# Key-norm roots on ACT, expert masks in pairs, and other small DVE and POOL instructions replaced, in a two-layer decoder block with its own instruction planner

## The chip, the cores and the metric

The kernel runs on one core of a Trainium2 chip. The core's engines work side by side, each through its own queue in order: TensorE (PE in the profile, with PEld for its weight loads), VectorE (DVE), ScalarE (ACT), GpSimd (POOL) and SyncE (SP, which here only issues DMAs). The metric is the device time of one execution in microseconds, lower is better. Before the change it was 1558.11 us, the median of three runs (1554.93, 1558.11 and 1562.21 us).

## The reference

The input `x` is 4 x 512 tokens of width 128, `ctx` is 4 x 154 rows of width 128. Six sublayers follow one another, and each ends in a layer norm of (input + sublayer):

```
x = LN(x + attn1(x))            # 16 heads of width 8, gated weights, softmax over 512 keys
x = LN(x + xattn(ctx, x))       # 16 heads of width 64, keys = LN(ctx) rows and LN(x) rows, 666 keys
x = LN(x + moe0(x))             # 16 experts of width 64, the best two, plus a shared expert
x = LN(x + delta(x))            # delta rule, 16 heads of width 64:
                                #   K = K / max(norm(K), 1e-12)
                                #   W += beta * (v - W k) k^T ; o = W q, token by token
x = LN(x + cross(x, ctx, mask)) # one head, 154 masked keys
x = LN(x + moe1(x))             # 8 experts of width 512, the best one: sum over e of mask_e * gelu(x W1[e] + b1[e])
                                #   then @ Wo + bo + x, an inner layer norm, and the outer one
```

A softmax needs the maximum of its scores subtracted; a matrix product in full precision is made here of three fast products of high and low parts.

## The kernel before, in words

The whole kernel is a program for a planner that stands in the kernel itself (class `_Plan`, lines 127 to 564). The sublayer functions do not issue instructions. They record operations, each with an engine, a cost in the planner's own model, the tiles that it reads and writes, and a rank. `run` (line 363) then goes through them like a list scheduler: for the engine whose next operation could start soonest it takes the operation with the lowest key (ready time plus `RANK` times the rank, plus `TILING` where PE would have to change the shape of its tile, plus `TABLE` where ACT would have to load another function table), places its tiles in arenas of SBUF and PSUM, and issues it. So the order on every queue comes out of costs, ranks, capacities (`cap`, line 1983) and the sizes of the arenas (`SB`, `SR`, line 735). The tables `R1` to `HOLD` (lines 1916 to 1981) hold one rank per piece of work. `keep_up` (line 506) puts a filler matmul (line 2042) where the planner sees PE idle or little used. Operations recorded as `pl.any` go to whichever of two engines can start them first.

The sublayers overlap. Seen from PE, the run has five stages: attn1 of the first batch with little else (about 0 to 160 us), attn1 and the cross attention attn2 of the four batches (160 to 850 us), moe0 and the start of the delta rule (850 to 1000 us), the delta rule with the cross layer (1000 to 1400 us), and moe1 at the end.

The places that the change touches, with their lines before:

- `two_parts` (line 793). A row's maximum is subtracted inside the score product, as two bf16 parts (high part and rest). DVE makes them with three reductions over small SBUF tiles. `attn1` (line 944) calls it 16 times; `attn2` (line 1174) calls it 32 times, after one more reduction that joins the maxima of the two halves of the keys.
- `few_k` (line 1157). Attn2's keys are 26 + 5 x 128. The 26 are handled apart, and DVE adds the high and low parts of 32 key columns for them, 32 times, both operands in SBUF.
- `norm` (line 782). For every layer norm DVE gathers mean and variance, POOL adds eps and takes the power -0.5 (`stats`, line 772), then POOL negates the mean and multiplies it by the root, and ACT applies scale and bias. There are 54 calls.
- `prepare` (line 1512). For each of the delta rule's eight units (128 tokens of two batches) POOL raises the squared key norms, 128x32 numbers, to the power 0.5; `phalf` is a tile of 0.5.
- `moe1` (lines 1865 to 1870). For each expert a small matmul spreads the token's mask over 128 partitions, and DVE multiplies it with the two parts of x (128x256 each). There are eight experts in eight half batches.

## Time and profile before

| | |
|---|---|
| profiled execution, device time | 1555.95 us |
| its span, first to last instruction | 1554.2 us |
| mean granted TensorE clock | 0.966 |
| PE busy | 1466.7 us, 94% |
| DVE busy | 1128.7 us, 73% |
| POOL busy | 893.6 us, 57% |
| ACT busy | 753.6 us, 48% |
| fillers on PE | 84 |
| function table loads on ACT | 8 |

The device time is 1.75 us above the span. Busy time of PE includes the fillers, and a matmul that runs at a lower granted clock counts as busy for longer. The rows by form give, for instructions of one shape, the total and the mean of one; their idle column is the time that the engine stood still just before them, with what ended it. Tiles of the planner's arenas have only the arena's name in the profile: `arena_sm` holds tiles of up to 64 numbers per partition, `arena_sr` the matmul operands in parts, `arena_sb` the rest, `arena_mr` weights first and other tiles later, `arena_ps` PSUM. Nearly all instructions carry the line of the planner's helper (L634), so the shape tells what they are.

### The profile page before, as it was taken

What the parts mean: (1) busy time and instruction counts of PE and PEld (TensorE: products, weight loads), DVE (VectorE), ACT (ScalarE), POOL (GpSimd) and SP (SyncE); (2) the same over time, 40 slices, a digit from 0 to 9 for tenths busy, and PEclk for the clock granted to TensorE, in tenths of its full rate; (3) what the DMA queues carried; (4) which work ended last, traced back from release to release, by engine and by line L of the source; (5) the groups of instructions that cost most, each with busy time, mean ns of one, the idle gap of its engine ahead of it and who ended that gap; (6) DMA issues with size and microseconds to landing.
All of it is one profiled execution on the core that took longest, in us unless ns stands there. A gap on an engine that the chain in (4) does not pass through costs nothing. (4 is left out here: it accounts for less than half of the span.)

```text
span 1554.2 us, 38252 instructions
## 1 busy us (share of the span) xinstructions
PE 1466.7 (94%) x15610; PEld 1004.8 (65%) x15610; DVE 1128.7 (73%) x2213; ACT 753.6 (48%) x1520; POOL 893.6 (57%) x1075
## 2 busy tenths in 40 slices
PE   6899999999999999999999998898999999999997
PEld 3355545545464454556544997787888788878886
DVE  6877787887678867677787777866776877665653
ACT  3657655665655756555455354253524444133311
POOL 6011465455574566578578547787787788761221
PEclk7878999999999999999999999999999999999999
DMA  3000001001010100002100607112322032210000
GB/s 117 9 22 8 8 9 37 1 16 36 1 37 1 26 27 15 23 4 89 29 29 2 139 2 164 42 32 44 57 57 47 13 57 57 52 47 5 8 8 11
DMA packets 106853, 53.84 MB, mean 35 GB/s; under 512 B 81261, under 2 KB 92525, under 8 KB 106677
## 3 DMA queue, kind: packets, MB, share of 16 engines
q1 hardware_dynamic: 106677, 51.40, 14.2%
q8 instruction: 122, 2.00, 0.5%
q14 instruction: 54, 0.44, 0.1%
HBM read 41.19 MB, written 10.09 MB: 33 GB/s over the span
## 5 line engine op out<-in xcount | busy, mean ns | idle before, releaser
L634 PE MATMUL arena_ps<-arena_sr 128*128 128x256 f32 (+6 forms) x3824 | 607.9, 375 | 31.7 <-DVE arena_sm L634 11.8
L634 PE MATMUL arena_ps<-arena_sb 64*64 64x64 f32 (+11 forms) x7744 | 579.6, 310 | 23.3 <-issue 5.9
L610 POOL TENSOR_TENSOR arena_sb<-arena_sb 128x1024 f32<-128x1024 f32 (+3 forms) x210 | 399.2, 1910 | 313.0 <-ACT arena_sb L634 191.6
L634 PEld LDWEIGHTS arena_ps<-arena_sr 128*128 128x128 f32 (+2 forms) x3824 | 417.1, 191 | 235.5 <-DVE arena_sm L634 65.5
L634 ACT ACTIVATE arena_sb<-arena_ps 128x512 f32<-128x512 f32 (+1 forms) x758 | 389.8, 571 | 263.8 <-PE arena_ps L634 249.1
L634 DVE TENSOR_REDUCE arena_sm<-arena_ps 128x2 f32<-128x668 f32 (+3 forms) x392 | 364.6, 952 | 103.3 <-PE arena_ps L634 98.3
L634 PEld LDWEIGHTS arena_ps<-arena_sb 64*64 64x64 f32 (+6 forms) x7648 | 337.7, 141 | 147.8 <-issue 88.6
L634 POOL TENSOR_TENSOR arena_sb<-arena_sb 128x30 f32<-128x30 f32 (+15 forms) x422 | 216.0, 512 | 32.4
L596 ACT COPY arena_sb<-arena_ps 128x512 f32<-128x512 f32 (+3 forms) x237 | 134.5, 575 | 184.2 <-PE arena_ps L634 163.4
L634 DVE TENSOR_TENSOR arena_sr<-arena_ps,arena_sr 128x256 fp32r<-128x256 f32 (+3 forms) x240 | 101.2, 464 | 53.6 <-PE arena_ps L634 45.5
L634 POOL TENSOR_SCALAR arena_sm<-arena_sm 128x2 f32<-128x2 f32 (+3 forms) x116 | 26.5, 228 | 193.2 <-DVE arena_sm L634 163.7
L634 DVE TENSOR_TENSOR arena_sb<-arena_ps,arena_sb 128x512 f32<-128x512 f32 (+3 forms) x133 | 83.1, 654 | 53.9 <-PE arena_ps L634 46.8
L634 PE MATMUL arena_ps<-arena_sr,arena_mr 128*128 128x512 f32 (+2 forms) x384 | 95.7, 383 | 0.8 <-DVE arena_sr L634 0.4
L634 DVE TENSOR_TENSOR arena_sb<-arena_ps,arena_sm 64x512 f32<-64x512 f32 (+1 forms) x116 | 77.7, 685 | 25.4 <-PE arena_ps L634 19.9
L634 PE MATMUL arena_ps<-arena_sb,arena_sm 64*128 64x512 bf16 (+2 forms) x512 | 90.4, 440 | 1.3 <-DVE arena_sb L598 0.5
L634 PEld LDWEIGHTS arena_ps<-arena_sr,arena_mr 128*128 128x128 f32 x384 | 64.2, 195 | 16.7 <-issue 5.1
L634 ACT CAST arena_sr<-arena_ps 128x334 fp32r<-128x334 f32 (+3 forms) x112 | 49.3, 463 | 45.0 <-PE arena_ps L634 44.4
L598 DVE COPY arena_sb<-arena_ps 128x512 f32<-128x512 f32 (+2 forms) x73 | 47.2, 648 | 30.4 <-PE arena_ps L634 28.9
L610 DVE TENSOR_TENSOR arena_sb<-arena_sb 128x1024 f32<-128x1024 f32 (+3 forms) x37 | 54.6, 1479 | 18.7 <-POOL arena_sb L610 8.8
L610 POOL TENSOR_TENSOR arena_sr<-arena_sb,arena_sr 128x512 fp32r<-128x512 f32 (+2 forms) x30 | 47.7, 1597 | 34.4 <-ACT arena_sr L634 23.9
L634 POOL TENSOR_TENSOR arena_sm<-arena_sm,phalf 128x32 f32<-128x32 f32 x8 | 43.5, 5441 | 23.1 <-ACT arena_sb L596 17.4
L634 ACT ACTIVATE x_in<-arena_sb,arena_sm 128x128 f32<-128x128 f32 x80 | 35.0, 487 | 44.8 <-POOL arena_sm L634 38.2
(113 smaller groups left out, 1237.6 us busy)
## 6 DMA issues: line engine op xcount, KB each, us to landing
arena_sb<-s_cd SPq DMA_DIRECT2D x20, 256.0 KB
arena_sb<-s_ald SPq DMA_DIRECT2D x7, 512.0 KB
s_td<-arena_sb SPq DMA_DIRECT2D x7, 512.0 KB
arena_mr<-s_cd SPq DMA_DIRECT2D x12, 256.0 KB
s_ald<-arena_sb SPq DMA_DIRECT2D x20, 128.0 KB
arena_sb<-s_td SPq DMA_DIRECT2D x20, 128.0 KB
arena_sb<-in_f_w_dram SPq DMA_DIRECT2D x4, 512.0 KB
s_ald<-arena_mr SPq DMA_DIRECT2D x12, 128.0 KB
```

The costliest lines, as they stand in the source:

```text
L596: nc.scalar.copy(dst.real(), src.real())
L598: nc.vector.tensor_copy(dst.real(), src.real())
L610: eng.tensor_tensor(dst.real(), x.real(), y.real(), op)
L634: f(*(v.real() if isinstance(v, _View) else v for v in args), **{k: v.real() if isinstance(v, _View) else v for k, v in kw.items()},)
```

## The change

- `two_parts` becomes a copy to bf16 and a subtraction. Attn2's joining of maxima becomes one minimum of two negated tiles, so its four reductions become three instructions, and attn1's three become two.
- `few_k` is copied by ACT out of PSUM, from the same product that the key parts are made of.
- In `norm`, POOL's two last steps become one DVE instruction.
- The root of the key norms is ACT's `Sqrt`, followed on DVE by one Newton step: a reciprocal, a product, a sum, a half. `Sqrt` needs a function table of its own.
- The masks of two experts share a PSUM bank, and one DVE product of 128x512 takes the place of two of 128x256.
- The planner gets other weights (`RANK`, `TILING`, `OTHER`), arena sizes, ranks and capacities throughout.

```diff
-    TABLES = {AF.Exp: ("exp",), AF.Gelu: ("gelu",), AF.Tanh: ("exp", "gelu")}
+    TABLES = {AF.Exp: ("exp",), AF.Gelu: ("gelu",), AF.Tanh: ("exp", "gelu"), AF.Sqrt: ("sqrt",)}
...
-    RANK, TILING, TABLE, OTHER = 0.1, 0.3, 0.7, 20
+    RANK, TILING, TABLE, OTHER = 0.05, 0.1, 0.7, 5.5
...
-    phalf = const.tile([P, 2 * H], F32, tag="phalf", name="phalf")
-    nc.gpsimd.memset(phalf, 0.5)
...
-    SB, SR, MR, SM = 27520, 13312, 8704, 512
+    SB, SR, MR, SM = 28416, 12416, 8704, 512
...
     def norm(dst, src, n, rows=P, eps=1e-5):
         mv, rs = stats(src, n, rows, eps)
-        nm, nb = pl.tile([P, n], name="nmean"), pl.tile([P, n], name="nb")
-        G_.tensor_scalar(nm[:rows, :], mv[:rows, :, 0], -1.0, None, ALU.mult)
-        G_.tensor_tensor(nb[:rows, :], nm[:rows, :], rs[:rows, :], ALU.mult)
+        nb = pl.tile([P, n], name="nb")
+        V_.scalar_tensor_tensor(nb[:rows, :], mv[:rows, :, 0], -1.0, rs[:rows, :], ALU.mult, ALU.mult)
...
-    def two_parts(dst, at, q):
+    def two_parts(dst, at, x):
 
-        V_.tensor_reduce(dst[..., at], q[..., 0:1], AX.X, ALU.add, part=True)
-        V_.tensor_reduce(q[..., 1], dst[..., at : at + 1], AX.X, ALU.add, negate=True)
-        V_.tensor_reduce(dst[..., at + 1], q, AX.X, ALU.add, part=True)
+        V_.tensor_copy(dst[..., at], x)
+        V_.tensor_tensor(dst[..., at + 1], x, dst[..., at], ALU.subtract)
...
                 V_.tensor_tensor(kn[:, 1, ks], pk, kn[:, 0, ks], ALU.subtract)
+                if i == 0:
+                    S_.copy(few_k[:, j, :], pk[:, 0:32])
...
-            V_.tensor_tensor(few_k[:, j, :], kn[:, 0, 0:32], kn[:, 1, 0:32], ALU.add)
...
-                    V_.tensor_reduce(m2[:, qt, :, i], sm, AX.X, ALU.max)
-            mx = pl.tile([P, NT, 2, 2], name="s2_mx")
-            V_.tensor_reduce(mx[:, :, :, 0], m2, AX.X, ALU.max, negate=True)
+                    V_.tensor_reduce(m2[:, i, qt, :], sm, AX.X, ALU.max, negate=True)
             mb = MB[p % 2]
+            mx = pl.tile([P, NT, 2], name="s2_mx")
+            V_.tensor_tensor(mx, m2[:, 0], m2[:, 1], ALU.min)
             two_parts(mb, 0, mx)
...
-        G_.tensor_tensor(
-            nk.rearrange("p i u m -> p (i u m)"), sm.rearrange("p i u m -> p (i u m)"), ph_, ALU.pow
-        )
+
+        root, over = (pl.tile([P, 2, 2, 8], name=f"s4_{x}") for x in ("root", "over"))
+        S_.activation(root, sm, AF.Sqrt)
+        V_.reciprocal(over, root)
+        V_.tensor_tensor(over, over, sm, ALU.mult)
+        V_.tensor_tensor(nk, over, root, ALU.add)
+        V_.tensor_scalar(nk, nk, 0.5, None, ALU.mult)
...
-            pl.at(rank[1])
-            pm = pl.bank([P, T // 2], f"s6_pm{b}", "pm6")
-            mm_(pm, f["sel8"][:, e * P : (e + 1) * P], ohT[0:8, :], start=True, stop=True)
-            mh, ml = (pl.tile([P, T // 2], F32R, f"s6_m{x}", f"m6{x}") for x in "hl")
-            V_.tensor_tensor(mh, pm, x2[0], ALU.mult)
-            V_.tensor_tensor(ml, pm, x2[1], ALU.mult)
+            if e % 2 == 0:
+                pl.at(rank[1])
+                pm = pl.bank([P, 2, T // 2], f"s6_pm{b}", "pm6")
+                with pl.group():
+                    for u in range(2):
+                        s8 = f["sel8"][:, (e + u) * P : (e + u + 1) * P]
+                        mm_(pm[:, u, :], s8, ohT[0:8, :], start=True, stop=True)
+                both = [pl.tile([P, 2, T // 2], F32R, f"s6_m{x}", f"m6{x}") for x in "hl"]
+                for m_, x in zip(both, x2):
+                    V_.tensor_tensor(m_, pm, bc_mid_(x, 2), ALU.mult)
+            mh, ml = (m_[:, e % 2, :] for m_ in both)
...
-    SPARE = 2048
+    SPARE = 0
     pl.cap(
...
```

Left out of the diff are the new values of the rank tables `R1` to `HOLD` (all of them change) and of the capacities in `cap` (22 of them, among them `CB` 2 to 4, `kn` and `z` 4 to 6, `tp` and `TN` 1 to 2, `KN` 3 to 2).

## The prediction

> **What bounds the kernel now.** First I read the page: the busy table, and the busy tenths with the granted clock below them.
>
> ```profile
> span 1554.2 us, 38252 instructions
> PE 1466.7 (94%) x15610; PEld 1004.8 (65%) x15610; DVE 1128.7 (73%) x2213; ACT 753.6 (48%) x1520; POOL 893.6 (57%) x1075
> ...
> PEclk7878999999999999999999999999999999999999
> ```
>
> PE bounds it. What can be won without less PE work is 1554.2 - 1466.7 = 87.5 us of idle time, the 84 fillers (27.7 us busy), and the time lost to a low granted clock, which lies in the first four slices. Then I asked for the same table by stage (columns: busy time of PE, PEld, DVE, ACT, POOL, then the clock).
>
> ```profile
> 0.00:160.00 160.00, 138.87 (x712) 70.04 (x712) 118.86 (x188) 91.45 (x173) 39.66 (x77) 0.81 0.14 38
> 160.00:850.00 690.00, 672.37 (x4544) 355.87 (x4542) 523.76 (x847) 405.23 (x788) 422.42 (x241) 0.99 0.08 22
> 850.00:1000.00 150.00, 134.67 (x1340) 120.40 (x1338) 115.88 (x300) 60.92 (x139) 93.82 (x138) 0.97 0.41 89
> 1000.00:1400.00 400.00, 377.81 (x7952) 333.42 (x7951) 287.35 (x581) 154.34 (x325) 308.66 (x549) 0.98 0.22 45
> 1400.00:1540.00 140.00, 137.93 (x1033) 120.29 (x1032) 79.90 (x287) 39.25 (x91) 26.78 (x66) 1.00 0.03 8
> ```
>
> PE idles for 21 us in the first stage, 18 in the attention stage, 15 in the middle, 22 in the delta stage, 2 in moe1, and 9 in the tail behind it. POOL has its fullest stage in delta (77%). Third, PE's waits: whom it waited for, total us, times, longest.
>
> ```profile
> PE arena_ps L634 <- DVE arena_sm L634: 15.3, 30, 2.7
> PE arena_ps L634 <- DVE arena_sb L634: 11.4, 36, 1.5
> PE arena_ps L634 <- ACT arena_sb L634: 8.4, 20, 1.0
> ...
> PE arena_ps L634 <- POOL arena_sb L610: 4.3, 8, 2.1
> ```
>
> So small work can reach the end only through waits of this size. Last, the rows by form that the change touches.
>
> ```profile
> L634 DVE TENSOR_TENSOR arena_sr<-arena_ps,arena_sr 128x256 fp32r<-128x256 f32 x152 | 55.1, 416 | 44.4 <-PE arena_ps L634 42.8 <-ACT arena_sr L634 1.0
> ...
> L634 DVE TENSOR_TENSOR arena_sb<-arena_sr 128x32 f32<-128x32 f32 x32 | 22.8, 712 | 0.0
> ...
> L634 DVE TENSOR_REDUCE arena_sb<-arena_sm 128x8 bf16<-128x16 f32 x32 | 6.1, 190 | 0.9
> ...
> L634 POOL TENSOR_TENSOR arena_sm<-arena_sm,phalf 128x32 f32<-128x32 f32 x8 | 43.5, 5441 | 23.1 <-ACT arena_sb L596 17.4 <-DVE arena_sm L634 4.4 <-ACT arena_sb L634 1.3
> ...
> L634 ACT ACT_TABLE_LOAD x8 | 10.3, 1283 | 2.2 <-PE arena_ps L634 1.3 <-PEq L2119 0.8
> ```
>
> The second and third rows matter most. A sum of 32 columns with both operands in SBUF takes 712 ns (748 in the attention stage), a reduction of 16 columns right beside it 190. POOL's 128x1024 sums (2388 ns each, POOL 61% busy there) run at the same time, so the first kind of instruction stands still for some 0.55 us and the second does not.
>
> **The change part by part.** The sum is made against the profiled execution, 1555.95 us (span 1554.2 and 1.75 around it), which is 2.2 us below the median 1558.11.
>
> *Work of each engine.* POOL loses eight powers (43.5 us), 54 negations of 0.22 to 0.23 us and 54 products of 0.19 to 0.26 (23 together): 67 us. ACT gains 32 small copies and eight roots at 0.23 us (the 128x32 row) and ten more table loads (18 in the new program) at 1.283: 22 us. DVE loses the 32 sums (22.8), the reductions of the parts (16 x 0.625 and 32 x 0.712, from rows of 166 to 225 ns: 32.8) and 128 mask products (53.3): 109 us. It gains 64 mask products at 0.683 (the 128x512 row): 43.7; eight Newton steps of 0.351 + 2 x 0.204 + 0.240 us: 8.0; 54 products for the norms at 0.22 (the 128x32 form) to 0.54 (the 128x4 form with a scalar): 12 to 29; and 128 copies, differences and minima of small SBUF tiles. Those are bounded by 0.17 us (an uncovered 128x16 product) and 0.75 (the blocked sum): 22 to 96 us. DVE thus ends between 23 us less and 68 us more. I take 0.45 us for each, as a third of them fall where POOL is nearly idle: about 58, so DVE gains some 18 us net. The name of the change isn't what DVE's rows say.
>
> *First stage.* Six calls of the parts and two norms stand before batch 0 reaches attn2, with DVE at 74% and POOL at 25%, so mostly uncovered: 6 x (0.625 - 0.34) + 2 x 0.25 = 2.2 us less, and PE's 8.4 us of waits for `arena_sm` there are of this chain. I take -2 (0 to -4).
>
> *Attention stage.* PE waits for DVE 6.6 us of its 17.6 idle, and DVE has 166 us to spare. A blocked small instruction delays the score reductions queued behind it; these free the one PSUM pair of `sm2`, for which PE's next scores wait. The same holds for a norm's product that now waits on DVE for POOL's power (0.57 to 1.04 us); the nearest row, DVE's waits for POOL's roots in the last stage, gives 0.65 each, or 35 us of DVE over all 54 if nothing stood ahead. I take +2 (-7 to +24).
>
> *Middle.* In the new order 53 fillers stand in four runs where 36 stood in two; 21 took 4.71 us. PE has a longer hole there: +4 (0 to +8). What is late next is the delta rule's first unit.
>
> *Delta stage.* The key norms' way to the first product shortens from 5.44 us on POOL to about 1.5 (root, reciprocal, two products, a half; the table load can run before its input is there). Before, the first mask matmul stands behind 9463 other matmuls of the work proper, after the last delta product (9447). After, it stands behind 9057, and the last delta product is the 9703rd: dense moe1 work moves into the stage where PE has 22 us of idle time and 25 fillers (about 6 us). That bounds the gain at 28; I take half, -14. Against it stands ACT's table switching: the PSUM copies queued behind a root wait up to 1.28 + 0.23 + 1.28 us. PE waits 4.9 us for ACT there now: +1 (0 to +13).
>
> *moe1 and the tail.* PE waits 1.3 us in 140, so nine us off DVE are hidden by PE itself. The last norm loses about 0.2 us: -0.7 in all.
>
> *Order.* The number of changes of tile shape on PE goes from 853 to 970. Eight attn1 products of one shape (128*32) follow each other's start by 1.00 us and sixteen by 1.85, so a run of one shape carries 0.15 us that isn't streaming: at worst 117 x 0.15 = 17.6 us. But the planner's price for staying in a shape fell from 0.3 to 0.1 us, so each change stands in the place of a wait of 0.1 to 0.3. I take 0 (-17 to +17). No DMA is added or removed; several move past one another on SP, whose share stays small.
>
> Sum: -2 + 2 + 4 - 14 + 1 - 0.7 = -9.7 us, which gives **1546 us**, 0.8% below the median.
>
> *Two rules against the rows.* The Trainium skill (SBUF — State Buffer, "Who interferes with whom") says that DVE and GpSimd lock one port pair for a whole instruction, that a reduction never needs it, and that two SBUF inputs do. The blocked sum and the free reduction agree, and it speaks against replacing reductions. By it the copies may escape, and the slow case below would lose a third of its 65 us, half of that at PE: about 1557. The skill (ScalarE: Activation LUTs, "What ACT_TABLE_LOAD costs") gives 2.66 us per switch, a drain included. Here a load takes 1283 ns and the next instruction starts within 20 ns of its end. By the page ACT would gain 14 us more, and the sum, if a tenth of it reached PE, 1 us.
>
> **The rivals.** *Hidden* (0.30): the work was off PE's path. For it: in the delta stage PE's waits name DVE and ACT, not POOL, and the rest of PE's idle is spread over pieces below 1 us. Then only the first stage, the middle and the tail count: 1555.95 - 2 + 4 - 0.7 = 1557 us.
>
> *Slower by the port* (0.22): in the attention stage the 116 small instructions outside the first stage cost 0.56 us more each (65 us), less the 17 that go with the 32 sums: 48 us of blocked DVE. Its place is the reductions behind them. If half shows as PE's waits, +24 in place of +2: 1568 us. It decides from about 40% on (19 us). Against it: the 32 blocked sums of now leave PE with only 6.6 us of waits for DVE, and the planner models this wait.
>
> **How the numbers follow.** Forecast 0.48, hidden 0.30, port 0.22. About 0.5% (7.8 us) can be told from no change here, so faster is below 1550.3 and slower above 1565.9: chances 0.48, 0.30 and 0.22. The low end, 1528, is the forecast with the delta gain at its bound (14 more) and 4 of the order's 17; the high end is the port case, 1568. The likeliest case's own range is 1528 to 1550.
>
> **What would show it.** Right: PE idle in the delta stage falls by over 10 us, POOL shows no 5.4 us powers, the 128x16 copies and differences take over 0.4 us in the attention stage, moe1's masks begin well before the last delta product. Wrong: the attention stage lasts over 700 us with waits for DVE above 20; or ACT's table loads show up as PE's waits above 10; or the first stage keeps a clock far from 0.81, which I leave as it is.

## The result and the profile after

The changed kernel takes 1577.93 us (median of four runs, 1574.67 to 1578.95) against 1560.16 us for the kernel before (median of four). The ratio is 1.0114 with a 95% interval of 1.0080 to 1.0148: about 18 us slower, where 1546 us had been forecast. A second series on another occasion gave 1575.88 against 1555.84 us, ratio 1.0127 (1.0106 to 1.0148). The profiled execution of the changed kernel took 1578.91 us.

The page of the changed kernel, its busy table and the granted clock in 40 slices:

```profile
span 1577.2 us, 38161 instructions
PE 1492.5 (95%) x15642; PEld 1009.6 (64%) x15642; DVE 1173.6 (74%) x2167; ACT 759.6 (48%) x1556; POOL 820.4 (52%) x960
...
PEclk7687999999999999999989999999999999999999
```

The span grew by 23.0 us, PE's busy time by 25.8. PE's idle time therefore did not grow; it fell from 87.5 to 84.7 us. POOL lost 73 us, as the change says. DVE gained 45 us, though the change is meant to take work off it. Next, the table by stage (busy time of PE, PEld, DVE, ACT, POOL, then the clock):

```profile
0.00:160.00 160.00, 132.56 (x631) 64.77 (x631) 115.82 (x168) 78.65 (x152) 36.33 (x67) 0.75 0.14 38
160.00:850.00 690.00, 675.91 (x4451) 350.62 (x4450) 539.15 (x780) 398.24 (x805) 391.80 (x214) 0.98 0.08 23
850.00:1000.00 150.00, 140.85 (x1360) 112.66 (x1359) 111.91 (x293) 71.61 (x155) 74.57 (x97) 0.98 0.29 64
1000.00:1400.00 400.00, 377.40 (x7806) 331.55 (x7804) 308.38 (x614) 164.16 (x331) 283.62 (x517) 0.97 0.24 52
```

The first stage runs at a clock of 0.75 instead of 0.81, and PE idles there 27 us instead of 21. Between 1000 and 1400 us PE idles 22.6 us where it idled 22.2; but the delta rule itself has moved, from 916.4 to 1378.1 us before (first to last 64x64 product) to 953.4 to 1400.8 after, and between these marks PE's idle time fell from 35.6 to 26.1 us. So the loss is made ahead of the delta rule, which begins 37 us later, a part of that because other work now stands ahead of it. About half of it lies in the first stage: attn2's first key projection starts at 145.5 us instead of 135.4, with 524 matmuls of the work proper ahead of it where there were 533. PE's waits (total us, times, longest):

```profile
PE arena_ps L634 <- DVE arena_sm L634: 17.4, 35, 3.1
PE arena_ps L634 <- DVE arena_sb L634: 14.3, 32, 1.7
...
PE arena_ps L634 <- DVE arena_sr L634: 5.3, 5, 3.8
```

Over all rows of this view, waits for DVE rose from 41.4 to 45.3 us, those for ACT fell from 13.9 to 6.8, those for POOL from 5.5 to 1.7. The new small instructions in the rows by form:

```profile
L634 DVE TENSOR_TENSOR arena_sb<-arena_sm,arena_sb 128x8 bf16<-128x8 f32 x32 | 19.7, 616 | 0.7
L634 DVE CAST arena_sb<-arena_sm 128x8 bf16<-128x8 f32 x32 | 19.4, 608 | 0.7
L634 DVE TENSOR_TENSOR arena_sm<-arena_sm 128x8 f32<-128x8 f32 x32 | 18.9, 590 | 0.9
L634 DVE TENSOR_TENSOR arena_sb<-arena_sm,arena_sb 128x16 bf16<-128x16 f32 x16 | 13.2, 825 | 0.3
L634 DVE CAST arena_sb<-arena_sm 128x16 bf16<-128x16 f32 x16 | 10.8, 672 | 0.2
```

The 128 copies, differences and minima take 82.0 us together, 0.64 us each. By these means they stand still beside POOL's sums, the copies (one SBUF operand) as much as the others: a single copy takes between 0.16 and 2.38 us. The obvious story is that this makes the kernel slower. The experiments show that in this kernel's order it does not.

### The profile page after: what moved, and what is told of

It is laid out like the page before. It is cut to its first block, busy times and chain, and to the rows that moved or that the text cites. A ratio compares the mean times of both kernels' runs of the same rounds, so it can differ in the third digit from the quotient of the medians.

```text
span 1577.2 us, 38161 instructions
## 1 busy us (share of the span) xinstructions
PE 1492.5 (95%) x15642; PEld 1009.6 (64%) x15642; DVE 1173.6 (74%) x2167; ACT 759.6 (48%) x1556; POOL 820.4 (52%) x960
## 3 DMA queue, kind: packets, MB, share of 16 engines
q1 hardware_dynamic: 106677, 51.40, 13.5%
HBM read 41.19 MB, written 10.09 MB: 33 GB/s over the span
## 4 chain that ended last, share of the span: by engine, by line
PE 72%; DVE 14%; issue 4%; DMA 3%; ACT 3%; POOL 1%; SPq 1%; POOLq 0%; DVEq 0%; ACTq 0%
PE arena_ps L634 71%; DVE arena_sm L634 6%; DVE arena_sb L634 5%; ACT arena_sb L634 2%; DVE arena_sr L634 1%; SPq L634 1%; ACT arena_sb L596 1%; POOL arena_sm L634 1%; DVE arena_sb L598 1%; POOL arena_sb L610 1%; DVE arena_sb L610 1%; DVE arena_mr L634 0%; DMA arena_sm<-s_25sd 0%; DMA arena_sb<-in_ctx_dram 0%; PE arena_ps L2049 0%
## 5 line engine op out<-in xcount | busy, mean ns | idle before, releaser
L634 PE MATMUL arena_ps<-arena_sr 128*128 128x256 f32 (+6 forms) x3824 | 615.4, 379 | 28.2 <-DVE arena_sm L634 15.3
L634 PE MATMUL arena_ps<-arena_sb 64*64 64x64 f32 (+11 forms) x7712 | 567.7, 311 | 18.5 <-DVE arena_sb L634 5.0
L634 PEld LDWEIGHTS arena_ps<-arena_sr 128*128 128x128 f32 (+2 forms) x3824 | 417.7, 193 | 250.6 <-DVE arena_sm L634 82.9
L610 POOL TENSOR_TENSOR arena_sb<-arena_sb 128x1024 f32<-128x1024 f32 (+3 forms) x206 | 385.9, 1884 | 332.2 <-ACT arena_sb L634 172.4
L634 ACT ACTIVATE arena_sb<-arena_ps 128x512 f32<-128x512 f32 (+1 forms) x755 | 387.1, 574 | 300.1 <-PE arena_ps L634 274.8
L634 DVE TENSOR_REDUCE arena_sm<-arena_ps 128x2 f32<-128x1024 f32 (+3 forms) x392 | 364.4, 953 | 93.9 <-PE arena_ps L634 89.5
L634 PEld LDWEIGHTS arena_ps<-arena_sb 64*64 64x64 f32 (+6 forms) x7616 | 323.4, 141 | 140.8 <-issue 89.2
L596 ACT COPY arena_sb<-arena_ps 128x512 f32<-128x512 f32 (+4 forms) x229 | 128.6, 570 | 185.9 <-PE arena_ps L634 165.4
L634 POOL TENSOR_TENSOR arena_sb<-arena_sb 128x30 f32<-128x30 f32 (+10 forms) x362 | 186.2, 514 | 27.9
L634 DVE TENSOR_TENSOR arena_sr<-arena_ps,arena_sr 128x512 fp32r<-128x512 f32 (+3 forms) x176 | 96.1, 578 | 54.0 <-PE arena_ps L634 19.9
L634 POOL TENSOR_SCALAR arena_sm<-arena_sm 128x2 f32<-128x2 f32 (+3 forms) x62 | 14.4, 234 | 206.0 <-DVE arena_sm L634 192.0
L634 DVE TENSOR_TENSOR arena_sb<-arena_ps,arena_sb 128x512 f32<-128x512 f32 (+4 forms) x133 | 83.0, 653 | 38.8 <-PE arena_ps L634 35.4
L634 PE MATMUL arena_ps<-arena_sr,arena_mr 128*128 128x512 f32 (+2 forms) x384 | 100.7, 390 | 4.1 <-DVE arena_sr L634 3.8
L634 PE MATMUL arena_ps<-arena_sb,arena_sm 64*128 64x512 bf16 (+2 forms) x512 | 89.6, 449 | 0.0
L634 DVE TENSOR_TENSOR arena_sb<-arena_ps,arena_sm 64x512 f32<-64x512 f32 (+1 forms) x113 | 75.2, 685 | 15.9 <-PE arena_ps L634 12.5
L634 PEld LDWEIGHTS arena_ps<-arena_sr,arena_mr 128*128 128x128 f32 x384 | 64.0, 196 | 26.7 <-issue 13.4
L598 DVE COPY arena_sb<-arena_ps 128x512 f32<-128x512 f32 (+3 forms) x84 | 55.2, 665 | 31.4 <-PE arena_ps L634 28.8
L634 ACT CAST arena_sr<-arena_ps 128x334 fp32r<-128x334 f32 (+3 forms) x112 | 50.6, 465 | 45.7 <-PE arena_ps L634 45.1
L634 ACT ACTIVATE x_in<-arena_sb,arena_sm 128x128 f32<-128x128 f32 x80 | 35.0, 488 | 62.8 <-DVE arena_sm L634 62.2
L634 PE MATMUL arena_ps<-arena_mr,arena_sb 32*32 32x32 f32 (+5 forms) x856 | 56.1, 247 | 4.3 <-issue 3.8
```

Of the source, the lines that this page charges most:

```text
L596: nc.scalar.copy(dst.real(), src.real())
L598: nc.vector.tensor_copy(dst.real(), src.real())
L610: eng.tensor_tensor(dst.real(), x.real(), y.real(), op)
L634: f(*(v.real() if isinstance(v, _View) else v for v in args), **{k: v.real() if isinstance(v, _View) else v for k, v in kw.items()},)
```

## The experiments

Two theories were set against each other. *Port*: the new small instructions stand still beside POOL's sums and make PE wait. *Order*: the new order of all queues, with its new weights, ranks and capacities, costs the time, whatever the instructions are. So most kernels keep one of the two orders exactly and exchange only what a recorded operation issues. The planner's costs and placements stay as they are; a helper replaces the calls of the last recorded operation:

```diff
+    def emit(*calls):
+        pl.ops[-1].calls[:] = [lambda _, c=c: c() for c in calls]
```

Two limits of this go with every result below. In the old order an exchanged instruction stands at the queue place of the one that it replaces, and the planner did not know its cost; no run planned the new instructions with the old weights and ranks. And the masks in pairs were put back in no run, nor was ACT's copy in the new order, so both are part of what is called the new order here.

All ratios below are to the kernel before, run beside on the same chip. "Old order" is that of the kernel before, "new order" that of the changed kernel.

| run | order | what differs from that order's own kernel | median us | ratio (95%) |
|---|---|---|---|---|
| a1 | new | nothing | 1575.88 | 1.0127 (1.0106 to 1.0148) |
| e1 | old | new parts of the maxima | 1618.61 | 1.0414 (1.0388 to 1.0440) |
| e2 | new | old parts | 1574.28 | 1.0121 (1.0100 to 1.0142) |
| e3 | old | all edits but the masks | 1634.95 | 1.0503 (1.0474 to 1.0531) |
| e4 | old | norms' product and root | 1581.12 | 1.0147 (1.0126 to 1.0168) |
| e16 | old | norms' product | 1557.36 | 1.0019 (1.0002 to 1.0036) |
| e17 | old | root | 1569.99 | 1.0094 (1.0071 to 1.0117) |
| e5 | new | old parts and old norms | 1578.51 | 1.0134 (1.0111 to 1.0156) |
| e9 | new | old root (POOL's power) | 1600.12 | 1.0279 (1.0252 to 1.0307) |
| e13 | new | no root, no table loads for it | 1571.98 | 1.0121 (1.0096 to 1.0145) |
| e6 | new | start's POOL differences left out | 1574.54 | 1.0092 (1.0071 to 1.0114) |
| e12 | new | POOL's 1024-column sums in four pieces | 1574.57 | 1.0131 (1.0104 to 1.0157) |
| e7 | old | new parts, and the pieces | 1578.10 | 1.0119 (1.0100 to 1.0137) |
| e10 | old | the pieces | 1562.95 | 1.0037 (1.0016 to 1.0057) |
| e8 | old | key columns' sums as reductions | 1554.47 | 0.9995 (0.9973 to 1.0016) |
| e11 | old | both of these | 1563.04 | 1.0044 (1.0025 to 1.0064) |
| e14 | new | no fillers | 1577.40 | 1.0145 (1.0120 to 1.0171) |
| e15 | old | no fillers | 1561.29 | 1.0049 (1.0031 to 1.0067) |

**The parts, in both orders (e1, e2, and the changed kernel again).**

```diff
# e1, in the old order: the first and third reduction issue the new instructions, the second nothing
+        emit(lambda: nc.vector.tensor_copy(hi.real(), x.real()))
+        emit()
+        emit(lambda: nc.vector.tensor_tensor(lo.real(), x.real(), hi.real(), ALU.subtract))
# e2, in the new order: the other way round
+        emit(lambda: reduced(dst[..., at], q[..., 0:1]))
+        emit(lambda: reduced(q[..., 1], hi, negate=True), lambda: reduced(lo, q))
```

> The changed kernel as it is, as the yardstick of this chip for the other three. Both theories expect the 18 us over the kernel before that were measured already (1.008 to 1.015).

> The order of every engine is that of the kernel before; only the instructions of the maxima's parts are replaced by those of the changed kernel (one copy and one difference in place of three reductions, a minimum in place of the joining reduction: 128 small instructions whose operands lie in SBUF). Theory 'port': the loss of 18 us is these instructions standing still behind POOL's sums, with the score reductions queued behind them, so this kernel loses most of it: 1570 to 1580 us, DVE about 50 us busier than before, PE's waits for DVE up by 10 us or more. Theory 'order': the small instructions stand still here as well (mean 0.6 us against 0.2), but DVE has time to spare and the time stays within 5 us of the kernel before: 1555 to 1565.

> The order of every engine is that of the changed kernel; only the maxima's parts and their join are made by the reductions of the kernel before (rows of 166 to 225 ns there). All else of the change stays. Theory 'port': 10 us or more come back, 1560 to 1568 us. Theory 'order': DVE gets some 50 us less busy and the time hardly moves, 1573 to 1578 us, with the start-up as late as in the changed kernel (first scores at 29 us, first attn2 scores at 150).

Both theories were half right. In the old order the same 128 instructions cost 63 us, three times what the whole change costs. In the new order, taking them out again saves 1 us, within the uncertainty, although DVE falls from 1173.6 to 1125.2 us. The groups of PE that read these parts (the transposes that bring them into place) show why; in these rows by form the idle time before the group is what counts. The kernel before:

```profile
L634 PE MATMUL arena_ps<-ident_b,arena_sb 128*128 128x128 bf16 x192 | 19.6, 228 | 2.9 <-DVE arena_sb L634 2.9
```

The same row of e1 (L805 is the difference):

```profile
L634 PE MATMUL arena_ps<-ident_b,arena_sb 128*128 128x128 bf16 x192 | 20.6, 236 | 40.8 <-DVE arena_sb L805 36.5 <-DVE arena_sr L634 3.7 <-DVE arena_sb L634 0.4
```

Of the changed kernel:

```profile
L634 PE MATMUL arena_ps<-ident_b,arena_sb 128*128 128x128 bf16 x192 | 19.5, 230 | 2.9 <-DVE arena_sb L634 2.0 <-DVE arena_sm L634 0.7
```

And of e2:

```profile
L634 PE MATMUL arena_ps<-ident_b,arena_sb 128*128 128x128 bf16 x192 | 19.3, 228 | 2.7 <-DVE arena_sb L801 1.5 <-DVE arena_sm L634 0.9
```

In the old order PE waits 40.8 us for the parts, in the new one 2.9, with instructions that stand still for as long. The new order has other PE work between, as at this place of the changed kernel, where the difference takes 2.24 us and the transposes behind it wait for nothing (timeline: start, us):

```profile
302.68 4.82 POOL L610 TENSOR_TENSOR arena_sb<-arena_sb 128x1024 f32<-128x1024 f32 x2 [3.43 <-ACT arena_sb L634]
...
305.32 2.24 DVE L634 TENSOR_TENSOR arena_sb<-arena_sm,arena_sb 128x8 bf16<-128x8 f32 x1
...
306.62 0.96 PE L634 MATMUL arena_ps<-arena_sr,arena_mr 128*128 128x512 f32 x3
...
307.52 1.06 PE L634 MATMUL arena_ps<-arena_sb 128*32 128x512 f32 x8
...
308.52 0.40 PE L634 MATMUL arena_ps<-ident_b,arena_sb 128*128 128x128 bf16 x4
```

One such wait in e1, from the timeline (start, us; L1181 is the minimum, L801 the copy, L805 the difference):

```profile
401.64 5.89 POOL L610 TENSOR_TENSOR arena_sb<-arena_sb 128x1024 f32<-128x1024 f32 x3 [3.33 <-ACT arena_sb L634]
402.83 1.20 DVE L1181 TENSOR_TENSOR arena_sm<-arena_sm 128x8 f32<-128x8 f32 x1
...
404.07 1.20 DVE L801 CAST arena_sb<-arena_sm 128x8 bf16<-128x8 f32 x1
405.31 2.27 DVE L805 TENSOR_TENSOR arena_sb<-arena_sm,arena_sb 128x8 bf16<-128x8 f32 x1
...
407.64 0.40 PE L634 MATMUL arena_ps<-ident_b,arena_sb 128*128 128x128 bf16 x4 [3.43 <-DVE arena_sb L805]
```

Three POOL sums run back to back and end at 404.01, 405.23 and 407.53 us; the three small instructions end 0.03 to 0.05 us behind them, one after the other, 4.7 us for what takes 0.6 us elsewhere. And here the wait is paid twice. The table by stretches of e1 around it shows the clock (the last column but two):

```profile
405.20:408.60 3.40, 0.96 (x9) 0.97 (x10) 3.37 (x3) 0.53 (x2) 3.40 (x3) 1.00 0.00 0
408.60:412.00 3.40, 3.40 (x17) 3.40 (x16) 1.20 (x4) 1.61 (x5) 0.17 (x1) 0.50 0.00 0
412.00:415.40 3.40, 3.40 (x29) 2.25 (x29) 2.23 (x3) 1.99 (x5) 0.00 (x0) 1.00 0.00 0
```

A stretch in which PE was busy for 0.96 of 3.4 us is followed by one at half clock. In all, e1 has 41.8 us more idle time on PE than the kernel before and 48.3 us more of PE's work at half clock.

**Is it POOL's sums that hold them? (e7)** The same kernel as e1, with every POOL sum of 1024 columns issued as four of 256.

```diff
+            if e == "POOL" and dst.free == 1024:
+                for j in range(0, 1024, 256):
+                    ...
+                    eng.tensor_tensor(d[c], u[c], v[c], op)
```

> The order of the kernel before with the new parts (1618.6 us as such), and every sum or difference of 1024 columns on POOL issued as four of 256. The work is the same, POOL's is longer: by the 128x256 row four take 2.95 us in place of 2.39. Theory 'port': a small DVE instruction stands still until the POOL instruction beside it ends, so with pieces it waits a quarter as long: the copies and differences of 128x8 fall from 0.56 to 0.69 us to 0.4 or less, PE's waits of up to 3.9 us behind them go, and half or more of the 63 us comes back: 1565 to 1590 us. Theory 'queue': POOL keeps what it holds from one instruction to the next, or the 63 us have another cause than the small instructions' standing still: 1610 us or more.

By the ratios (1.0414 to 1.0119) some 45 of the 63 us came back. The rows by form of e7 (L813 the difference, L809 the copy, L1189 the minimum):

```profile
L813 DVE TENSOR_TENSOR arena_sb<-arena_sm,arena_sb 128x8 bf16<-128x8 f32 x32 | 17.9, 559 | 0.9
L809 DVE CAST arena_sb<-arena_sm 128x8 bf16<-128x8 f32 x32 | 15.0, 469 | 0.9
...
L1189 DVE TENSOR_TENSOR arena_sm<-arena_sm 128x8 f32<-128x8 f32 x32 | 13.1, 411 | 2.1 <-POOL arena_sm L642 1.1
...
L616 POOL TENSOR_TENSOR arena_sb<-arena_sb 128x256 f32<-128x256 f32 x428 | 303.7, 746 | 145.0 <-ACT arena_sb L642 137.9 <-PE arena_ps L642 6.7
```

In e1 these took 693, 564 and 925 ns. They do not fall to 0.2 us, but the long ones of over 2 us go, and PE's idle time before the transposes falls from 40.8 to 13.5 us. So the standing still beside POOL is real and costs most of the 63 us in the old order, and how long it lasts goes with the length of the POOL instruction beside it.

**All edits but the masks, in the old order, and the rest one by one (e3, e4, e16, e17).** The norms' product and the root are exchanged in the same way (e4 both, e16 and e17 one each); e3 has them, the parts and the copy of the key columns by ACT.

```diff
# norm
         G_.tensor_scalar(nm[:rows, :], mv[:rows, :, 0], -1.0, None, ALU.mult)
+        emit()
         G_.tensor_tensor(nb[:rows, :], nm[:rows, :], rs[:rows, :], ALU.mult, also=mv)
+        emit(lambda: nc.vector.scalar_tensor_tensor(nb.., mv.., -1.0, rs.., ALU.mult, ALU.mult))
# root, in place of POOL's power
+        emit(
+            lambda: nc.scalar.activation(root, sm.real(), AF.Sqrt),
+            lambda: nc.vector.reciprocal(over, root), ...   # and three more on DVE
+        )
```

> The order of every engine is that of the kernel before, with all edits of the change but the masks two at a time: the new parts, the norms' product on DVE in place of two POOL instructions, the key norms' root by ACT's square root and a Newton step in place of POOL's power, and the 32 first key columns copied by ACT in place of the sum on DVE (this copy takes the high part alone, so the low part of those columns is left out; the instruction has the size of the changed kernel's). Theory 'port': 1568 to 1580 us. Theory 'order': within 6 us of the kernel before, 1553 to 1566. A third theory, table loads: if the square root's table switches (about 16 more loads of 1.28 us in an order that has no place for them) cost, ACT's loads and PE's waits for ACT show it, at most some 20 us, and mostly between 900 and 1400 us.

> The order of the kernel before, with two edits alone: the norms' product in one DVE instruction in place of two on POOL, and the key norms' root by ACT's square root and a Newton step in place of POOL's power. The maxima's parts stay reductions. The kernel with all edits but the masks stands 16 us above the one with the new parts alone; these two edits, or the 32 key columns copied by ACT, make that difference. Theory 'port': the norms' products stand still on DVE behind POOL's sums and their waits for POOL's power hold the queue: 1563 to 1576 us. Theory 'tables': the square roots' table switches hold ACT between 900 and 1400 us: 1560 to 1575, with PE's waits for ACT up by 5 us or more. If both are cheap: 1553 to 1560, and the 16 us are the copies' on ACT.

> The order of the kernel before, with the norms' product alone in one DVE instruction (13 of 128x4 that took 621 ns, 24 of 128x2 that waited 12 us for POOL in all, 17 smaller). Theory 'norm': a wait of the DVE queue for POOL's power, and what is queued behind it, carries the 22 us: 1570 to 1578. Theory 'root': within 5 us of the kernel before.

> The order of the kernel before, with the root alone: ACT's square root and the four Newton instructions on DVE in place of POOL's power, 15 more table loads (19 us of ACT). Theory 'root': the table loads and DVE's waits for the root (9.5 us in the run with both) carry the 22 us: 1570 to 1578. Theory 'norm': the shorter way to the key norms gains or changes little here: 1546 to 1558.

The parts cost 63 us, the root 15, the norms' product 3. All together with the copy by ACT cost 79, which leaves nothing for the copy (in e3 it takes the high part out of SBUF, not the sum out of PSUM). The root was forecast to gain. In the old order it loses, and the timeline of e17 at the second of the eight units shows how (L1525 is the square root, L1526 the Newton step's reciprocal):

```profile
937.31 0.35 DVE L634 RECIPROCAL arena_sm<-arena_sm 128x32 f32<-128x32 f32 x1
...
938.92 1.18 ACT L596 COPY arena_sb<-arena_ps 64x512 f32<-64x512 f32 x2 [2.30 <-PE arena_ps L634]
940.12 1.28 ACT L1525 ACT_TABLE_LOAD   x1
941.41 0.23 ACT L1525 ACTIVATE root<-arena_sm 128x32 f32<-128x32 f32 x1
...
941.67 0.35 DVE L1526 RECIPROCAL over<-root 128x32 f32<-128x32 f32 x1 [4.01 <-ACT root L1525]
...
947.25 1.87 PE L634 MATMUL arena_ps<-ident,arena_sm 128*16 128x128 f32 x8 [5.96 <-DVE arena_sm L634]
```

The squares are ready at 937.3 us. In ACT's queue two PSUM copies stand ahead of the root, and these wait for PE themselves; then the table is loaded. DVE's queue stands for 4.01 us meanwhile, with some twenty small instructions behind it that PE's next product needs. That product waited 2.65 us in the kernel before and waits 5.96 here. POOL's power, 5.4 us long, held nobody's queue, as POOL alone worked on it while DVE went on. Over all units DVE waits 10.8 us for the root, and PE idles 13.4 us more than in the kernel before.

**The new order with old pieces (e5, e9, e13).**

> The order of the changed kernel, with the maxima's parts as reductions again (as in the run that did this alone, 1574 us) and the norms' product on POOL in two instructions again. What is left of the change's instructions are the root on ACT, the masks two at a time and the key columns' copy. Theory 'order': the new order hides these instructions whatever their form, and the loss is its own: 1570 to 1578 us. Theory 'forms': the blocked instructions that were left (54 products on DVE) carry it: 1565 or less.

> The changed kernel in its order, with the key norms' root by POOL's power again (eight of 5.4 us, 43 us of POOL; ten table loads and the Newton steps go). In the order of the kernel before, root and norms' product cost 22 us, all of it behind 850 us. Theory 'order': the new order was laid out for the short root; with the power it waits longer for each unit's first product, so the time rises by 5 us or more: 1580 to 1600. Theory 'root': the root on ACT costs in the new order too, as it did in the old one, and going back brings 5 to 20 us: 1556 to 1571.

> The changed kernel, with ACT's square root replaced by a plain copy, so that the key norms are not roots (the root is left out) and the ten table loads that go with it fall away (12.8 us of ACT). Theory 'tables': the loads stand ahead of PSUM copies that PE waits for between 900 and 1400 us, and without them 5 us or more come back: 1571 or less. Theory 'order': ACT is at 41% there and hides them: 1573 to 1578.

With the parts and the norms put back the new order stays where it was. With POOL's power put back it loses another 24 us: PE idles 35 us between 1000 and 1400 us instead of 22.6. So the new order does live on the short root, as the old one lived on the power; with the power it is 43 us slower than the kernel before. The twelve table loads that go with the root (18 against 6) are hidden there: without root and loads the ratio is 1.0121 against 1.0127.

**The start of the new order (e6).** POOL's first three differences are replaced by a filling with zero.

```diff
             pl.any.tensor_tensor(lo, raw, hi, ALU.subtract)
+            pl.ops[-1].calls[:] = [lambda _, lo=lo: nc.gpsimd.memset(lo.., 0.0)]
```

> The changed kernel, with POOL's first three 128x1024 differences (the low parts of attn2's weights, 7.1 us from 18.8 us on) replaced by filling with zero, which reads no SBUF: the low parts of these weights are left out. In the changed kernel two DVE instructions of 128x128 take 2.35 and 2.42 us beside these differences (0.28 and 0.29 in the kernel before, where they ran earlier) and PE's first projections wait 3.8 us behind them. Theory 'start': those two fall to 0.3 us, the first scores go from 29 to 25 us or less, and with less time at the low clock 4 to 8 us of the loss come back: 1568 to 1572. Theory 'made up': DVE and PE of the first stage take the time back or lose it at the clock anyway, and the end moves by less than 2 us: 1573 to 1577.

The timeline of the changed kernel at the start:

```profile
18.84 7.08 POOL L610 TENSOR_TENSOR arena_mr<-arena_sb,arena_mr 128x1024 fp32r<-128x1024 f32 x3 [11.49 <-ACT arena_mr L634]
...
18.98 2.35 DVE L634 TENSOR_TENSOR arena_mr<-arena_sb,arena_mr 128x128 fp32r<-128x128 f32 x1 [6.02 <-ACT arena_mr L634]
...
21.26 2.42 DVE L634 SCALAR_TENSOR_TENSOR arena_sb<-arena_sb 128x128 f32<-128x128 f32 x1
23.60 0.68 DVE L634 TENSOR_TENSOR arena_sr<-arena_ps,arena_sr 128x512 fp32r<-128x512 f32 x1
...
24.43 2.90 PE L634 MATMUL arena_ps<-arena_sr,arena_mr 128*128 128x512 f32 x6 [3.84 <-DVE arena_sr L634]
```

The timeline of e6 at the same place:

```profile
17.91 0.29 DVE L634 TENSOR_TENSOR arena_mr<-arena_sb,arena_mr 128x128 fp32r<-128x128 f32 x1 [4.25 <-ACT arena_mr L634]
18.12 0.28 DVE L634 SCALAR_TENSOR_TENSOR arena_sb<-arena_sb 128x128 f32<-128x128 f32 x1
18.32 0.68 DVE L634 TENSOR_TENSOR arena_sr<-arena_ps,arena_sr 128x512 fp32r<-128x512 f32 x1
```

In the new order DVE's weight difference and bias land beside POOL's, 4.8 us instead of 0.57, and all projections come 5 us later. Without that the first scores start at 23.0 us instead of 29.1, attn2's first key projection starts at 140.4 instead of 145.5, and the ratio falls by 0.0035, some 5 us, though the two intervals just overlap and the medians, each with its own kernel before beside it, differ by 1.3 us only. This is one part of the order's 20 us that has a place. Which of two things does it is open: the fillings wait for no input and run at 7.4 to 10.1 us already, so POOL's queue behind them is free earlier too.

**Pieces and reductions elsewhere (e8, e10, e11, e12).** If standing still were dear in general, the kernel before should gain by having less of it.

```diff
# e8: the sum of a key's two parts as a reduction of the pair
+            emit(lambda f=.., k=..: nc.vector.tensor_reduce(f.real(), k.real().rearrange("p i n -> p n i"), AX.X, ALU.add))
```

> The kernel before, in its order, with one edit the other way round: the 32 sums of a key's high and low part (128x32, 712 ns each beside POOL's sums) become reductions of the pair, whose operands also lie in SBUF. Theory 'port': these fall to about 0.2 to 0.25 us, DVE gets 15 us less busy; they stand right ahead of the score reductions, so PE's waits for DVE fall and the kernel gains 2 to 8 us: 1551 to 1557. If the order hides them: within 2 us of the kernel before.

> The kernel before, in its order, with nothing but POOL's sums and differences of 1024 columns cut into four of 256. POOL gets some 62 us busier (255.6 + 62.5 us of such work rises to 304 + 76 by the rows of the run with pieces). Theory 'port': DVE's instructions with two operands in SBUF (the 128x32 sums at 712 ns above all) stand still for less, DVE falls by 15 to 30 us, and where PE waits for DVE some of it shows: 1545 to 1557. If POOL's longer work is what counts: 1562 or more.

> Both edits of the two runs before on the kernel before: the key columns' sums as reductions, and POOL's sums in four pieces. Theory 'port': the gains do not add in full, as the pieces already shorten the sums' standing still (416 ns in the run with pieces): 1545 to 1556, at most 3 us better than the better one of the two.

> The changed kernel, with POOL's sums and differences of 1024 columns cut into four of 256. In the order of the kernel before this brought back 40 of the 63 us that the new parts cost there; that kernel itself, which has few such instructions, lost 7 us by it. Theory 'order': nothing in the new order waits on the small instructions any more but the start (5 us by the run without the start's differences), and POOL's longer work costs some 7: 1572 to 1582. Theory 'port': standing still costs elsewhere too: 1570 or less.

The 32 sums fell from 712 to 209 ns, as the row by form of e8 shows,

```profile
L1162 DVE TENSOR_REDUCE arena_sb<-arena_sr 128x32 f32<-128x64 f32 x32 | 6.7, 209 | 0.5 <-ACT arena_sr L634 0.5
```

and the time did not move. With pieces DVE falls by 28 us in the old order, and the time rises by 6; in the new order it falls by 41 (to 1132.7 us), and the time stays. Each order hides the standing still that it was laid out for, so taking it away brings nothing. No run beat the kernel before.

**The fillers (e14, e15).** `pl.filler` issues nothing.

> The changed kernel without its 116 fillers (matmuls of a constant into a free PSUM bank, which nothing reads; 38.4 us of PE's busy time). Theory 'fillers take time': the 32 more of them than before stand partly ahead of work proper, and without them the time falls by 5 us or more: 1570 or less. Theory 'fillers save time': they stand where PE would be idle, and without them more of PE's work runs at half clock: 1580 to 1610 us, with the clock of the profiled run below 0.95.

> The same for the kernel before: without its 84 fillers (27.7 us of PE's busy time). Theory 'fillers take time': down by up to 5 us, 1550 to 1556. Theory 'fillers save time': up by 5 to 30 us, less than in the new order if the new order has more idle places to fill.

In the old order the fillers save 7.6 us by the ratio; in the new one, 32 more of them save nothing that can be measured (1.0145 against 1.0127) and cost nothing either. The first theory, that they take time, is out.

**Where the 20 us are.** For each profiled execution the trace gives PE's idle time, and its record of the granted clock (1 or 0.5, in stretches of 3.4 us and multiples) gives the part of PE's busy time that lies in half-clock stretches. All in us, each from one execution:

| | span | PE idle | PE busy | of it at half clock | fillers busy |
|---|---|---|---|---|---|
| before | 1554.2 | 87.5 | 1466.7 | 87.6 | 27.7 |
| after | 1577.2 | 84.7 | 1492.5 | 123.9 | 38.4 |
| after again (a1) | 1574.1 | 85.9 | 1488.2 | 110.2 | 38.6 |
| e1 | 1616.9 | 129.3 | 1487.6 | 135.9 | 26.9 |
| e9 | 1599.8 | 105.7 | 1494.1 | 122.3 | 37.9 |
| old order without fillers (e15) | 1558.4 | 104.7 | 1453.7 | 104.5 | 0 |
| new order without fillers (e14) | 1579.6 | 107.5 | 1472.1 | 100.5 recorded, about 130 by the durations | 0 |

Over the 18 profiled executions with fillers (ten of the old order, eight of the new), PE's busy time is 1430.1 us in the old order and 1442.1 in the new, plus 0.424 us for each us of work at half clock. This is a least-squares fit; the rest scatters by 1.8 us, the slope's standard error is 0.035, that of the 12.0 us between the orders 1.0. So the second profile of the changed kernel reads: 12.0 us more PE time at equal clock, of which up to 10.9 is the fillers' own busy time, 9.6 us ((110.2 - 87.6) x 0.424) by the low clock, and 1.6 us less idle time, 20.0 together, against a span that is 19.9 us longer. In the first profile the clock's share is 15.4 and the sum 24.6, against 23.0.

The clock differs from run to run, and these two pairs overstate its share. Over all runs on record the mean granted clock is 0.965 in the kernel before (81 runs) and 0.960 in the changed one (nine runs). That is 108 and 126 us at half clock; with PE busy in some 0.87 of it, as in these profiles, the clock's share is an estimated 7 us of the 20 (18 x 0.87 x 0.424).

That is an account, not yet a cause. Without fillers the pair differs by 21 us too, so the fillers' busy time isn't what the order costs. In that pair the clock has to be read with care, as e14's record of it lacks a stretch. Here are the table of the same 33 us in e14 and in a1, and the first products of one form in each (rows by form from 22.8 to 32 us in e14, from 24.6 to 33.5 us in a1), e14 first both times:

```profile
24.00:57.00 33.00, 29.37 (x110) 15.96 (x108) 25.26 (x38) 13.00 (x25) 11.44 (x19) 1.00 0.00 1
24.00:57.00 33.00, 29.70 (x102) 16.92 (x106) 25.55 (x43) 12.01 (x23) 13.22 (x19) 0.50 0.00 1
...
L634 PE MATMUL arena_ps<-arena_sr,arena_mr 128*128 128x512 f32 x10 | 5.3, 669 | 5.9 <-DVE arena_sr L634 5.9
L634 PE MATMUL arena_ps<-arena_sr,arena_mr 128*128 128x512 f32 x10 | 5.3, 669 | 3.6 <-DVE arena_sr L634 3.6
```

The record of e14 says full clock, but its matmuls last as long as a1's at half clock: 669 ns, where the same form takes 421 ns in e14 from 90 to 116 us. Until about 55 us the groups have a1's half-clock durations. With these 29 us counted as half clock, the 21 us of the pair without fillers are an estimated 11 us of low clock, 3 of idle time, and some 8 of more PE time at equal clock. What makes the last part isn't known. More changes of tile shape (967 in that trace against 854) are a candidate that no run changed alone. They can hardly carry much, as the pair with fillers has as many more of them, and there the 12.0 us at equal clock are mostly the fillers' own.

## Why the prediction was wrong

The forecast of 1546 us, and its range up to 1568, missed a measured 1578. By its own steps:

- **"Order. ... I take 0 (-17 to +17)" is the step that failed.** With the parts, or the parts and the norms, put back, the new order still stands at 1.0121 and 1.0134, some 20 us above the kernel before. The bound was made of tile-shape changes alone, and its middle was put at zero. It had no term for more work at half clock, which is an estimated 7 us over all runs. It left the clock of the first stage "as it is"; its own list of what would prove it wrong names a first-stage clock far from 0.81, and it came to 0.75. The prediction counted the new fillers only in the middle. There are 10.7 us more of them in all, but without any the order costs as much. Which of the new weights, ranks, capacities and arena sizes makes the loss stays open.
- **First stage, -2.** It became later instead: attn2's first key projection starts at 145.5 us instead of 135.4. Some 5 of these 10 us are made at the start (140.4 us in e6), where two DVE instructions of the old kind, which the diff does not touch, were moved beside POOL's differences. The prediction priced the edited instructions and not the neighbours that the new order gives to the others.
- **Attention stage, +2 (-7 to +24).** In the order that was run, putting the parts back changes the time by -1 us, so the value taken was near, and the rival *Slower by the port* is not what happened. Its mechanism is real, though, and was priced too low: it took half of the blocked time for PE's loss. In the old order 45 us more on DVE cost 63 us, as 41.9 us of idle time plus the lower clock after it. What hid it in the changed kernel is the order, which the prediction named ("the planner models this wait").
- **DVE's 18 us net.** They were 45. The 128 small instructions took 82.0 us, not 58; 0.64 us each against 0.45 taken, inside the bounds of 0.17 to 0.75. The copies do not escape, as the prediction thought they might.
- **Delta stage, -14 (bound 28).** The mechanism was right, in the order that was run. From its first to its last 64x64 product the delta rule takes 447.4 us instead of 461.7, with 9.5 us less idle time on PE, no powers of 5.4 us are left, and the first masks start 21.6 us before the last delta product where they started 14.0 us behind it. With the power put back, the new order loses 24 us (e9). But this gain needs the edit and the order together: in the old order the same short root costs 15 us, as it holds DVE's queue. And it was added to an order term of zero, where the new order loses more ahead of the delta rule. The prediction's counts of matmuls ahead of the first mask stand in no trace; by the traces 14396 matmuls of the work proper stood ahead of it and 13615 do now, the way that it said.
- **Middle, +4; table loads, +1; moe1 and tail, -0.7.** PE's idle time between 850 and 1000 us fell from 15.3 to 9.1 us. The loads cost nothing in the new order (e13). These were small and stayed small.
- **The rival *Hidden*** (1557 us) is what e16 and e8 show for single edits, not for the whole.

The sum took the old trace's instructions one by one and held the order at zero mean. With a planner in the kernel, the edits' price in the old order (79 us without the masks) and what the new order takes back of it (59) are both several times the net, and the old trace shows neither. That the forecast of the attention stage came near its mark is in part luck, as the order hid a price that was put too low.

## What to carry to other kernels

When an edit comes with a new order of the queues, keep the old order and exchange only the instructions, and the other way round; here that split the net of 20 us into +79 and -59, which no reading of either profile gave. The split depends on the way: beginning with the new order, the order with POOL's power costs 43 us and the short root takes 24 of them back. A small instruction on DVE beside long GpSimd sums costs what its consumer's slack leaves of the sum's length, so either give the consumer other work or cut the sums into pieces, which itself costs time where nothing waited (6 us in e10). And an ACT step put into a chain of small DVE work can hold the whole DVE queue, where a much longer GpSimd step beside it held nobody.

## What the runs showed of the hardware

- A copy with its only operand in SBUF (128x8 float32 to bf16) stands still beside POOL's sums like an instruction with two: 608 ns on average in the changed kernel, up to 2.38 us. A reduction of 128x64 stays at 209. The Trainium skill (SBUF — State Buffer, "Who interferes with whom") allows for this, as it lists copies and casts among the operations that can take the shared ports in their fast modes, and it says that a GpSimd instruction which only writes does not hold back a DVE instruction with two SBUF inputs. The second agrees with e6, where a DVE instruction of the bias's form (128x128, L634) takes 0.29 us at 9.65 us, in the midst of POOL's third filling (9.14 to 10.09 us), against 2.42 us beside POOL's difference in the changed kernel.
- Beside POOL sums cut into pieces the small DVE instructions wait for less: the longest of the 128 takes 1.30 us in e7 and 2.36 in e1. The pieces cost POOL 746 ns each, four take 2.98 us where one sum took 2.39.
- A wait of PE can be paid again by the clock. In e1 stretches at half clock follow stretches in which PE was busy for 0.96 of 3.4 us, and also for 2.31 of 3.4 (before 377.9 us). But one in the kernel before follows 3.38 of 3.4 (before 500.3 us), so PE's busy time in the trace alone does not tell which waits do it. By the fit, each us of PE's work at half clock cost 0.42 us. The Trainium skill (TensorE: Matmul & The Clock Gate, "What's actually happening") puts the fall to half clock after at least one idle window of about 3.4 us; the length of the stretches agrees, but the windows given here were not idle.
- Another load of an ACT table takes 1283 ns in every order and number (6, 8, 18 and 23 loads).
